# A transformer layer in one kernel: transposes as 12-bit products, and another order table for the attention

## The chip, the cores and the metric

The kernel runs on one core of a Trainium2 chip. A core has five engines that run side by side, each with its own instruction queue, and meet at semaphores: TensorE (PE in the profile; PEld is its weight load), VectorE (DVE), ScalarE (ACT), GpSimd (POOL) and SyncE (SP), which issues DMA transfers. The metric is the device time of one execution in microseconds (us); lower is better. Before the change it is 889.84 us, the median of three runs (888.79 to 892.21).

## The reference

The layer is a "macaron": half a feed-forward network, attention, another half feed-forward network, each on a layer-normalized input and added to the residual. All data is 32-bit.

```python
x = x + 0.5 * ffn(layernorm(x), w_gate, w_up, w_down)
x = x + attention(layernorm(x), Wq, bq, Wk, bk, Wv, bv, Wo, bo)
x = x + 0.5 * ffn(layernorm(x), w_gate, w_up, w_down)
```

x is (2, 1024, 256): two sequences of 1024 tokens with 256 channels. The feed-forward network has 1024 inner channels, silu(x Wg) * (x Wu); of every four neighbours the two largest in magnitude are kept before Wd. The attention is causal, with rotary positions, 32 query heads and 8 key/value heads of 8 channels each, so that four query heads share a key head:

```python
scores = einsum('bhqd,bhkd->bhqk', q, k_rep) / sqrt(8)
scores = where(kpos > qpos, -inf, scores)
out = einsum('bhqk,bhkd->bhqd', softmax(scores), v_rep)
```

## The kernel before

The time has three parts: the first feed-forward network with the projections of the first sequence beside it (up to about 210 us), the attention (to about 715 us), and the second feed-forward network.

**Units and rounds.** The attention works on 16 units, one for each sequence and key head (`units`, L701). A unit has four query heads and 1024 tokens. Each unit goes through two passes, and in round n of the loop `round_` pass 1 of unit n (`cur`) is mixed with pass 2 of unit n-1 (`prev`), and with the preparation of unit n+1 (`nxt`). So both kinds of work are there in rounds 1 to 15; round 0 has no pass 2 and runs beside the last part of the first feed-forward network, and round 16 has no pass 1.

**Precision.** Score products use the format that the kernel calls FR, with 12 bits[...]. To lose nothing, each query and key is split into a high part that the format holds and the remainder (`split`, and L446/L449 in `project`), and both are laid in the rows of one product. Tile `part` holds these parts, typed FR.

**prepare (step prep, L468).** Eight transposes by TensorE turn one unit's 80 columns of `part` (four query heads and a key head, two parts of 8 channels each) into rows, in the PSUM tile `hT`. ACT copies them to `stage`, and SP's DMA queue lays them into the rows of `qT` and `kT`: for each of two strips, zeros into two rows for the maxima, and sixteen copies of parts for both strips together. `qT` and `kT` are in three copies, used in turn.

**pass1 (steps p1, L511).** Score products with queries as rows of the output, `s` at L526, with K = 64 rows so that two heads run at once in the two halves of the array. On the diagonal, the causal mask is added as bf16 products (L534). DVE takes the negated maximum of each row (L546). A step has four heads, or with a second number only one pair of heads. An output of 1024 columns fills the PSUM tile, 128 x 2 x 512.

**negated and shift (neg1, and steps shift, L560).** The maxima are split into two 12-bit parts on POOL (`ms`); four transposes turn them into rows (`mT`, L565), ACT copies them (`mrow`), and four DMA transfers put them into `qT`, so that the score products of pass 2 come out with the maximum already subtracted. shift 0 serves the first half of a unit's queries, shift 1 the second half, in the next round. negated(0) comes after the last p1 step with a number below 4.

**pass2 (steps p2, L579).** Scores again, now with keys as rows (L590). ACT takes the exponential (L599), POOL clears the causal half on the diagonal (L602). **weighted (steps av, L613)** multiplies the exponentials in full 32 bits with the values and a column of ones (L622), summed up in the PSUM tile `av`; after the last step of a half ACT copies it (`oT`, L631). **normalize (steps norm)** transposes `oT` (L640) and divides by the sum of exponentials on DVE. After norm 1 of the last unit of a sequence, `output` applies Wo.

**What sets the order.** PE and POOL run in program order inside the attention (`manual_schedule`); that order is the table `order` (L688), written out by hand as 58 steps. A step number selects a (query tile, key block) in `steps1` or `steps2`. DVE, ACT and SP are ordered by the scheduler from it. Every fourth step of rounds from 1 on, a piece of the second sequence's projection is put in (`second`).

**Buffers.** PSUM has three tiles of two banks in turn (`ps_big`), shared by the p1, p2 and hT tiles and the projections; one of one bank (`ps_tr`) for the other transposes, and one (`ps_acc`) for av. The exponentials have seven buffers (`es`).

A transpose by TensorE takes the data as weights and streams a unit matrix `ident` through them, in 32 bits; its call is `nc.tensor.transpose`.

Of the kernel before, what the change touches and what calls it, by code (L numbers as in the profile page):

```python
# [8 lines left out]
FP = mybir.dt.float32  # L9
BF = mybir.dt.bfloat16  # L10
FR = mybir.dt.float32r
# [5 lines left out]
P = 128  # L17
B, T, C = 2, 1024, 256
NT = B * T
TB = 512  # L20
NTB = NT // TB
NTT = TB // P
# [3 lines left out]
REP = H // NKV  # L26
# [8 lines left out]
def macaron_kernel(  # L35
# [77 lines left out]

    ident = const.tile([P, P], FP, name="ident")
    make_identity(nc, ident)


    half_id = const.tile([P, 2, P], BF, name="half_id")
# [226 lines left out]
    def attention(actx, last, beside_first):  # L345
# [2 lines left out]


        qTs, kTs, vaugs, parts, attns = [], [], [], [], []  # L350
        zeros = ap1.tile([2, TB], FP, name="zeros")
        nc.vector.memset(zeros, 0.0)
        late = {}

# [102 lines left out]
        class Unit:  # L457
# [10 lines left out]
            def prepare(self):  # L468


                s = f"{self.b}_{self.g}"
                tr = ps_big.tile([P, 2, TB], FP, name=f"hT{s}", tag="big")
                src = parts[self.b][:, :, bass.ts(self.g, REP + 1), :].bitcast(FP)
                for t in range(NQT):
                    nc.tensor.transpose(  # L475
                        tr[0 : 2 * GW, t // NTT, bass.ts(t % NTT, P)],
                        src[:, t, :, :].rearrange("p h n -> p (h n)"),
                        ident,
                    )
                hT = ap1.tile([P, T], FP, name=f"stage{s}", tag="stage")  # L480
                nc.scalar.copy(hT[0 : 2 * GW, :], tr[0 : 2 * GW, :, :].rearrange("p i n -> p (i n)"))
                W = 2 * D
                for s in range(2):

                    lo = s * STRIP + ROWS
                    nc.sync.dma_start(
                        out=self.qT[lo : lo + 2, :, :].rearrange("p i (c n) -> p (i c) n", n=TB),
                        in_=zeros[:, None, :].to_broadcast([2, REP, TB]),
                    )
                    for j in range(2):  # L490
                        for i in range(2):
                            lo = s * STRIP + j * W + i * D
                            nc.sync.dma_start(
                                out=self.kT[lo : lo + D, :],
                                in_=hT[REP * W + j * D : REP * W + j * D + D, :],
                            )
                        lo = s * STRIP + j * W
                        for pair in range(2):
                            h = 2 * pair + s
                            nc.sync.dma_start(  # L500
                                out=self.qT[lo : lo + W, pair, :], in_=hT[h * W : h * W + W, :]
                            )
# [57 lines left out]
            def shift(self, half):  # L560
# [1 line left out]
                s = f"{self.b}_{self.g}_{half}"  # L562
                tr = ps_tr.tile([P, TB], FP, name=f"mT{s}", tag="tr")
                for t in range(NTT):
                    nc.tensor.transpose(  # L565
                        tr[0 : 2 * REP, bass.ts(t, P)],
                        self.ms[:, t, :, :].bitcast(FP).rearrange("p i k -> p (i k)"),
                        ident,
                    )
                mT = late["2"].tile([2 * REP, TB], FP, name=f"mrow{s}", tag="mrow")  # L570
                nc.scalar.copy(mT, tr[0 : 2 * REP, :])
# [114 lines left out]


        order = """  # L688
        neg1; p2 0 1; p1 3 1; p2 0 0; av 11; p1 9 0; shift 1; p1 0; p2 1 1; p1 3 0; p2 1 0;
        p1 4 1; norm 1; p2 2; prep; p1 2 1; p2 3; av 0; p2 4 0; p1 7; p2 4 1; av 1; p1 2 0;  # L690
        p2 5 0; p1 1; av 2; p2 5 1; p1 6 0; p2 6 1; av 3; p1 5; shift 0; p1 8 0; p2 6 0;
        p1 8 1; av 4; p2 7 1; p1 10 0; av 5; p2 7 0; p1 9 1; norm 0; p2 8 1; p1 11 0;
        p2 8 0; av 6; p2 9 1; p1 4 0; p2 9 0; av 7; p1 11 1; p2 10; p1 10 1; av 8; p2 11;
        p1 6 1; av 9; av 10
        """
        steps1 = [(qt, kc) for qt in range(NQT) for kc in range(qt // NTT + 1)]
        steps2 = [(qh, kb) for qh in range(2) for kb in range((qh + 1) * NTT)]
# [172 lines left out]
```

## Time and profile before

| | before |
|---|---|
| median of 3 runs | 889.84 us |
| the profiled execution | 894.08 us |
| its span (first to last instruction) | 892.3 us |
| PE busy, share of the span | 848.9 us, 95% |
| DVE busy | 664.8 us, 75% |
| ACT busy | 435.9 us, 49% |
| POOL busy | 220.3 us, 25% |
| mean granted clock of PE | 0.978 |
| hT transposes, 128 records | 19.1 us busy, 296 ns mean |
| mT transposes, 128 records | 19.6 us busy, 277 ns mean |

The profile is of one execution. An engine is busy while an instruction of it is under way. Records of matmuls overlap, since TensorE is a pipeline: a record of 273 ns may be followed by the next after 109 ns, so the time that a product costs is read from the starts of neighbours, not from its length. L12 is line 12 of the kernel before. In `qT<-mrow`, the tile written stands left of the arrow.

### The profile page before, as it was taken

How to read it: one execution, taken by the hardware profiler on the slowest of the kernel's cores; microseconds unless marked ns; L12 is line 12 of the kernel's file. 1: busy time of each engine (PE TensorE's matmuls, PEld its weight loads, DVE VectorE, ACT ScalarE, POOL GpSimd, SP SyncE). 2: the span in 40 equal slices, each digit the busy share in tenths (PEclk: the TensorE clock that was granted, in tenths of full speed). 3: DMA queues.
4: the chain of work that ended last, by engine and by line, in shares of the span. 5: the costliest groups of instructions: out<-in, count | busy, mean ns of one | idle time of the engine just before them, and what ended most of it. 6: DMA issues, size and time to landing. Idle time of an engine off the chain costs nothing.

```text
span 892.3 us, 14666 instructions
## 1 busy us (share of the span) xinstructions
PE 848.9 (95%) x5760; PEld 454.4 (51%) x5760; DVE 664.8 (75%) x927; ACT 435.9 (49%) x570; POOL 220.3 (25%) x405
## 2 busy tenths in 40 slices
PE   5999999898899989999998999999998899999998
PEld 2446664575444454445446444444443444555566
DVE  4797898878777877787885878788883157978682
ACT  1331223202666756777773777777777434212220
POOL 3002376320154433452221222222122200000000
PEclk9999999998899989999998999999998999999999
DMA  8100000201201210221120222112200000000001
GB/s 256 27 0 2 1 1 0 36 14 27 38 14 28 39 27 15 39 35 19 28 39 1 39 39 35 20 28 39 38 3 2 1 1 0 1 12 12 21 3 47
DMA packets 20819, 22.95 MB, mean 26 GB/s; under 512 B 11408, under 2 KB 15888, under 8 KB 20752
## 3 DMA queue, kind: packets, MB, share of 16 engines
q1 hardware_dynamic: 19136, 19.15, 11.6%
q10 hardware_dynamic: 1616, 2.88, 0.9%
q8 instruction: 45, 0.74, 0.4%
q14 instruction: 22, 0.18, 0.1%
HBM read 6.29 MB, written 2.10 MB: 9 GB/s over the span
## 4 chain that ended last, share of the span: by engine, by line
PE 76%; DVE 15%; ACT 4%; POOL 3%; issue 1%; DMA 1%; SPq 1%; ACTq 0%; POOLq 0%
PE gu L229 20%; PE av L622 14%; PE s L590 10%; PE o L284 10%; PE s L526 9%; DVE neg L546 5%; ACT e L599 2%; PE s L534 2%; PE oo L673 2%; PE hT L475 2%; PE otr L640 2%; DVE least L546 2%; PE pr L397 2%; PE mT L565 2%; DVE h L269 1%; PE lnT L180 1%
## 5 line engine op out<-in xcount | busy, mean ns | idle before, releaser
L599 ACT ACTIVATE e<-s 128x1024 f32<-128x1024 f32 (+1 forms) x320 | 291.8, 938 | 136.1 <-PE s L590 123.0
L546 DVE TENSOR_REDUCE least<-s 128x2 f32<-128x1024 f32 (+3 forms) x224 | 251.4, 1144 | 58.3 <-PE s L534 37.2
L622 PE MATMUL av<-e,vaug 128*32 128x512 f32 (+3 forms) x1536 | 162.7, 503 | 1.8 <-ACT oT L631 1.6
L590 PE MATMUL s<-qT,kT 64*128 64x512 f32 (+3 forms) x768 | 151.0, 419 | 9.7 <-DVE neg L546 4.7
L602 POOL TENSOR_SCALAR_AFFINE_SELECT e<-e 128x256 f32<-128x256 f32 (+1 forms) x192 | 94.5, 493 | 257.5 <-ACT e L599 257.2
L526 PE MATMUL s<-kT,qT 64*128 64x512 f32 (+3 forms) x768 | 140.4, 389 | 3.7 <-DVE least L546 1.7
L590 PEld LDWEIGHTS s<-qT,kT 64*128 64x128 f32 x768 | 68.8, 190 | 111.7 <-DVE least L546 40.3
L229 PE MATMUL gu<-xnT,wg_sb 128*128 128x512 f32 x256 | 123.6, 606 | 1.9 <-ACT xnT L187 1.2
L229 PE MATMUL gu<-xnT,wu_sb 128*128 128x512 f32 x256 | 120.5, 593 | 0.0
L546 DVE TENSOR_REDUCE neg<-s 128x2 f32<-128x1024 f32 (+1 forms) x96 | 97.9, 1042 | 28.7 <-PE s L534 26.9
L284 PE MATMUL o<-wd_sb,h 128*128 128x256 f32 x512 | 116.5, 382 | 0.2 <-DVE x L305 0.2
L284 PEld LDWEIGHTS o<-wd_sb,h 128*128 128x128 f32 x512 | 95.8, 190 | 18.4 <-issue 5.1
L526 PEld LDWEIGHTS s<-kT,qT 64*128 64x128 f32 x768 | 69.4, 187 | 58.0 <-ACT e L599 36.3
L237 ACT ACTIVATE sg<-gu 128x512 f32<-128x512 f32 x64 | 38.1, 595 | 111.2 <-PE gu L229 111.2
L240 ACT ACTIVATE a<-h 128x512 f32<-128x512 f32 x64 | 40.3, 630 | 98.1 <-DVE h L239 97.7
L229 PEld LDWEIGHTS gu<-xnT,wu_sb 128*128 128x128 f32 x256 | 49.0, 191 | 62.1 <-issue 62.1
L238 DVE TENSOR_TENSOR sg<-sg,gu 128x512 f32<-128x512 f32 x64 | 43.7, 684 | 48.8 <-ACT sg L237 48.8
L229 PEld LDWEIGHTS gu<-xnT,wg_sb 128*128 128x128 f32 x256 | 48.9, 194 | 56.5 <-issue 49.6
L622 PEld LDWEIGHTS av<-e,vaug 128*32 128x32 f32 x1536 | 32.0, 108 | 49.9 <-issue 26.5
L534 PE MATMUL s<-half_mask,half_id 64*128 64x128 bf16 (+1 forms) x1024 | 56.1, 209 | 0.0
L159 POOL TENSOR_TENSOR rstd<-ve,neg_half 128x4 f32<-128x4 f32 x12 | 12.3, 1025 | 155.4 <-DVE ve L157 155.3
L239 DVE TENSOR_TENSOR h<-sg,gu 128x512 f32<-128x512 f32 x64 | 43.9, 687 | 2.2
(75 smaller groups left out, 679.8 us busy)
## 6 DMA issues: line engine op xcount, KB each, us to landing
qT<-stage SPq DMA_DIRECT2D x128, 64.0 KB
kT<-stage SPq DMA_DIRECT2D x128, 32.0 KB
qT<-mrow SPq DMA_DIRECT2D x128, 4.0 KB
out<-x SPq DMA_DIRECT2D x8, 256.0 KB
wu_sb<-in_wu SPq DMA_DIRECT2D x2, 512.0 KB
wg_sb<-in_wg ACTq DMA_DIRECT2D x2, 512.0 KB
x<-in_x SPq DMA_DIRECT2D x2, 512.0 KB
wd_sb<-in_wd ACTq DMA_DIRECT2D x1, 1024.0 KB
```

The lines of the kernel that those rows point to most:

```text
L229: nc.tensor.matmul(out=gu[:, i, :], lhsT=w_sb[:, kc, gb, j, :], rhs=self.xnT[tb][:, kc, :], start=(kc == 0), stop=(kc == 1),)
L238: nc.vector.tensor_tensor(sg, sg, gu[:, 0, :], ALU.mult)
L239: nc.vector.tensor_tensor(h[:, j, :], sg, gu[:, 1, :], ALU.mult)
L240: nc.scalar.activation(a[:, j, :], h[:, j, :], AF.Abs)
L284: nc.tensor.matmul(out=o[:, i, :], lhsT=self.hms[tb][k // 4][:, k % 4, bass.ts(2 * t2 + i, P)], rhs=wd_sb[:, k // 4, k % 4, :], start=(k = ...
L526: nc.tensor.matmul(out=to[:, i, s, :], lhsT=self.qT[strip, pair, bass.ts(qt, P)].bitcast(FR), rhs=self.kT[strip, bass.ds(kc * TB, n)].bitc ...
L534: nc.tensor.matmul(out=to[:, i, s, n - P + lo : n], lhsT=half_id[strip, half, :], rhs=half_mask[strip, half, lo:], start=False, stop=(half ...
L546: ins = nc.vector.tensor_reduce(dst, to, AX.X, ALU.max, negate=True)
L590: nc.tensor.matmul(out=to[:, i, s, :], lhsT=self.kT[strip, bass.ts(kb, P)].bitcast(FR), rhs=self.qT[strip, pair, bass.ds(q0, n)].bitcast(F ...
L599: nc.scalar.activation(e, to, AF.Exp, scale=SCALE)
L602: nc.gpsimd.affine_select(out=e[:, :, :, 0:P], in_=e[:, :, :, 0:P], pattern=[[0, 2], [0, len(pairs)], [1, P]], compare_op=ALU.is_ge, fill=0.0,
L622: nc.tensor.matmul(out=self.av[32 * i : 32 * i + 32, TB - n : TB], lhsT=vaugs[self.b][:, kb, bass.ds(self.g * (D + 1), 32)], rhs=es[i], st ...
```

## The change

The transposes hT and mT become plain products in the 12-bit format with a unit matrix in that format, `ident_r`, copied once from `ident`. Their data is already rounded to that format, so the product with one is exact. The tile `zeros` shrinks to half its columns, and its DMA repeats it twice as often. The order table has the same 58 steps in another order.

```diff
     ident = const.tile([P, P], FP, name="ident")
     make_identity(nc, ident)
+    ident_r = const.tile([P, P], FR, name="ident_r")
+    nc.vector.tensor_copy(ident_r, ident)
...
-        zeros = ap1.tile([2, TB], FP, name="zeros")
+        zeros = ap1.tile([2, TB // 2], FP, name="zeros")
...
-                src = parts[self.b][:, :, bass.ts(self.g, REP + 1), :].bitcast(FP)
+                src = parts[self.b][:, :, bass.ts(self.g, REP + 1), :]
                 for t in range(NQT):
-                    nc.tensor.transpose(
-                        tr[0 : 2 * GW, t // NTT, bass.ts(t % NTT, P)],
-                        src[:, t, :, :].rearrange("p h n -> p (h n)"),
-                        ident,
+
+                    nc.tensor.matmul(
+                        out=tr[0 : 2 * GW, t // NTT, bass.ts(t % NTT, P)],
+                        lhsT=src[:, t, :, :].rearrange("p h n -> p (h n)"),
+                        rhs=ident_r,
+                        start=True,
+                        stop=True,
                     )
...
-                        out=self.qT[lo : lo + 2, :, :].rearrange("p i (c n) -> p (i c) n", n=TB),
-                        in_=zeros[:, None, :].to_broadcast([2, REP, TB]),
+                        out=self.qT[lo : lo + 2, :, :].rearrange("p i (c n) -> p (i c) n", n=TB // 2),
+                        in_=zeros[:, None, :].to_broadcast([2, 2 * REP, TB // 2]),
...
                 for t in range(NTT):
-                    nc.tensor.transpose(
-                        tr[0 : 2 * REP, bass.ts(t, P)],
-                        self.ms[:, t, :, :].bitcast(FP).rearrange("p i k -> p (i k)"),
-                        ident,
+                    nc.tensor.matmul(
+                        out=tr[0 : 2 * REP, bass.ts(t, P)],
+                        lhsT=self.ms[:, t, :, :].rearrange("p i k -> p (i k)"),
+                        rhs=ident_r,
+                        start=True,
+                        stop=True,
                     )
...
         order = """
-        neg1; p2 0 1; p1 3 1; p2 0 0; av 11; p1 9 0; shift 1; p1 0; p2 1 1; p1 3 0; p2 1 0;
-        p1 4 1; norm 1; p2 2; prep; p1 2 1; p2 3; av 0; p2 4 0; p1 7; p2 4 1; av 1; p1 2 0;
-        p2 5 0; p1 1; av 2; p2 5 1; p1 6 0; p2 6 1; av 3; p1 5; shift 0; p1 8 0; p2 6 0;
-        p1 8 1; av 4; p2 7 1; p1 10 0; av 5; p2 7 0; p1 9 1; norm 0; p2 8 1; p1 11 0;
-        p2 8 0; av 6; p2 9 1; p1 4 0; p2 9 0; av 7; p1 11 1; p2 10; p1 10 1; av 8; p2 11;
-        p1 6 1; av 9; av 10
+        neg1; p2 0 1; p1 1; p2 0 0; av 11; p1 0; shift 1; p1 3 1; p2 1 1; p1 9 0; av 0;
+        p2 1 0; p1 3 0; prep; p1 2 1; p2 2; p1 2 0; p2 3; norm 1; p2 4 0; p1 10 0; p2 4 1;
+        av 1; p1 10 1; p2 5 1; p1 7; p2 5 0; p1 11 0; shift 0; av 2; p2 6 1; p1 9 1; av 3;
+        p1 5; p2 6 0; p1 4 0; av 4; p2 7 1; p1 6 1; p2 7 0; av 5; p1 4 1; p2 8 0; av 6;
+        p2 8 1; p1 8 1; p2 9 0; norm 0; av 7; p2 9 1; p1 11 1; p2 10; av 8; p1 8 0; p2 11;
+        p1 6 0; av 9; av 10
         """
```

## The prediction

> **What bounds the kernel now.** I read the page's busy times first. TensorE (PE) is busy nearly throughout; VectorE (DVE) and ScalarE (ACT) are not.
>
> ```profile
> PE 848.9 (95%) x5760; PEld 454.4 (51%) x5760; DVE 664.8 (75%) x927; ACT 435.9 (49%) x570; POOL 220.3 (25%) x405
> ```
>
> Next, busy time in windows of 28 us over the attention, because the chain of waits repeats there with that period (its reductions at L546 stand at 521.54, 549.51 and 577.47).
>
> ```profile
> core 0: us, PE busy (x) PEld busy (x) DVE busy (x) ACT busy (x) POOL busy (x), PEclk, DMA share, GB/s
> 510.00:538.00 28.00, 27.52 (x288) 13.38 (x280) 22.77 (x26) 20.96 (x25) 6.79 (x17) 1.00 0.20 32
> 538.00:566.00 28.00, 27.51 (x288) 13.38 (x280) 22.79 (x26) 20.96 (x25) 6.81 (x17) 1.00 0.19 33
> 566.00:594.00 28.00, 27.52 (x288) 13.38 (x280) 22.76 (x26) 20.95 (x25) 6.76 (x17) 1.00 0.19 32
> ```
>
> A round of the attention, one pass of the order table, takes 28.0 us. PE has work in flight for 27.5 of it, at the full clock, while DVE has 5 us and ACT 7 us to spare. So a round is set by PE's stream of products and by what holds that stream up. Third, the timeline of one round (columns: start us, length us, engine, line, operation, tiles, count, wait before it):
>
> ```profile
> 535.17 0.39 PE L526 MATMUL s<-kT,qT 64*128 64x512 f32 x2
> 535.49 1.06 PE L622 MATMUL av<-e,vaug 128*32 128x512 f32 x8
> 536.48 0.44 PE L590 MATMUL s<-qT,kT 64*128 64x128 f32 x4
> 536.76 0.45 PE L526 MATMUL s<-kT,qT 64*128 64x512 f32 x2
> ...
> 540.47 0.60 PE L565 MATMUL mT<-ident,ms 128*8 128x128 f32 x4
> 541.00 0.44 PE L526 MATMUL s<-kT,qT 64*128 64x128 f32 x4
> ...
> 542.41 0.44 PE L590 MATMUL s<-qT,kT 64*128 64x384 f32 x2 [0.20 <-DVE neg L546]
> ...
> 544.25 1.07 PE L475 MATMUL hT<-ident,part 128*80 128x128 f32 x8
> 545.25 0.44 PE L526 MATMUL s<-kT,qT 64*128 64x384 f32 x2
> ```
>
> The reader is to see three things. The four mT transposes hold PE from 540.47 to 541.00, 0.53 us: one record is 0.273 long (the view of tile mT, below), so they start (0.60 - 0.273)/3 = 0.109 us apart, and 0.20 passes from the last start to the next product. The eight hT transposes take 1.00 us at the same spacing. And a real wait for a buffer: 542.41, where a p2 tile waits for a reduction.
>
> ```profile
> L565 PEld LDWEIGHTS mT<-ident,ms x128: 82/87/128, 204.5 to 678.7; 128*8 128x8 f32 x128
> L565 PE MATMUL mT<-ident,ms x128: 272/273/417, 204.7 to 678.8; 128*8 128x128 f32 x128
> ```
>
> (Smallest, median and largest duration in ns.) The fourth view is by form, in the draining round (681.75 to 682.0), where score products of 128 columns in the 12-bit format stand with nothing slow behind them:
>
> ```profile
> L590 PE MATMUL s<-qT,kT 64*128 64x128 f32 x4 | 0.3, 246 | 0.0
> ```
>
> They are two pairs (the two halves of the rows run at once); a mean of 246 ns hides 218 for the first pair and 273 for the second, and the pairs start 0.06 us apart (single records: 681.81 and 681.87).
>
> [...] weights of 12-bit products follow each other every 107 to 109 ns. [...]
>
> **The change, part by part.**
>
> *Transposes.* Each unit has 8 hT and 2 x 4 mT. mT now: 3 x 0.109 + 0.20 = 0.53. [...] gain 0.21, twice a unit 0.42. hT: [...] gain 0.31. [...] I take 0.73 us a round[...]. I prefer overlap because the 12-bit pairs at 508.6 and 508.7 start 108 ns apart with 107 ns loads[...].
>
> *Order, on PE.* The table holds the same 58 steps. What differs for PE is how often it goes from half-height products (64 rows, p1 and p2) to full-height ones (av, shift, norm, prep) and back. From the timeline: av follows a 512-column product after 0.32 where a product of its own kind follows after 0.23 (+0.09); the step back costs 0.54 from the last av start where the next av would come after 0.43 (+0.11); and the first half-height product has its weight load in the open (0.334 to the next, against 0.227: +0.107). So a visit costs 0.3. The old table has 16 visits a round (only av 9 and av 10 stand together), the new one 14, since shift 0 stands at av 2 and norm 0 at av 7. With some 0.03 to 0.1 for the change inside the pair I take 0.27 each, 0.54 a round.
>
> *Order, in waits.* The score tiles share three PSUM pairs in turn with hT, so each tile waits until the third before it has been read: by DVE (1.22 us for 1024 columns; 1.13 behind another), or ACT (1.02; 0.92 behind another). I walked both tables through a round with these lengths and the product spacings above (0.23, 0.17, 0.12, 0.11 a pair by width; masks 0.09 or 0.18; av 0.88, 0.67, 0.45, 0.24). The old table gives 27.5 us with 1.3 of waits, the largest at p2 1 0 (0.47; the trace has 0.37 there, the line at 542.41). The missing 0.5 are weight loads that waits leave in the open. The new table has 1.55 of waits, in the stretch from prep to p2 6 0, where only av 1 and the pair shift 0/av 2 break a run of score tiles: p2 2 0.19, p1 2 0 0.30, p1 7 0.17, p2 5 0 0.39. An example: p1 10 1 is done at 10.7 and its reduction, behind p1 10 0's, ends at 12.15; p2 5 0 needs that buffer and PE could start it at 11.8. With the old spacing of the transposes the new table walks at 27.5, as the old one. So the two visits saved are given back to waits, and only with the shorter transposes does the round fall, to 26.8.
>
> Net: 0.73 + 0.54 - about 0.57 given back (0.27 longer waits, and loads left in the open or shared with a wait) = 0.7 us a round. Both tables are complete in rounds 1 to 15: 15 x 0.7 = 10.5. hT of the first unit lies in the FFN, on the path: 0.3. Round 0 is bound by DVE (no exponentials, reductions alone); the draining round by ACT's exponentials and the landing of mrow: nothing, within 2 us either way, also for where norm 1 starts the output of the first sequence. Sum 11.
>
> *The rest at nothing.* The copy of the unit matrix (128 x 128, like attn's 0.29) stands on DVE ahead of xn, where DVE idles 1.21 for rstd; without that cover it costs 0.3 once. Zeros of half the width make twice as many packets on SP's queue, two issues of 0.65 a unit, ahead of shift 0's four mrow issues; those rows are wanted at the next round's start, 14 us later. shift 1's mrow is tighter: its landing is wanted by p2 4 0, 6.3 us after mT in the new table, 6.5 in the old; the trace has the last issue done 3.9 after mT's start, so 0.3 is free with a landing of 2.1. If it were late, everything on PE behind p2 4 0 waits. prep's loads have over 20 us. av 4 needs the copy of av 3's sum (0.59) with three steps between instead of five: it fits with nothing to spare, at most 0.3 a round.
>
> The profiled execution took 894.08 (span 892.3); less 11 it is 883. The median is 4.2 lower: 889.84 - 11 = 879.
>
> **Rivals.**
>
> *The waits do not grow.* DVE has 5 us spare in 28. Then 0.73 + 0.54 = 1.27 x 15 = 19 come through, 870. Against it: the run of score tiles in the middle.
>
> *The waits take it all.* If p2 and p1 in that stretch wait 0.5 more than walked, or loads and products of hT go in turn, a round gains under 0.25: 886 to 890.
>
> *Slower: narrow 12-bit products are slow.* [...] (av, 128 columns: two records of 0.11), the spacing would be 0.215: 16 x 0.106 = 1.7 more a round, 15 rounds 26, so 916. As the order alone gives nothing, it decides from a spacing of 0.109 on; at 0.127 the loss passes 0.5%. Against it: 536.48 to 536.76 holds two narrow pairs and an open load in 0.28.
>
> **How the numbers follow.** Forecast 0.50 (own range 874 to 885); waits not growing 0.22; waits taking all 0.17 (0.03 of it still faster by 0.5%, 0.01 slower); waits beyond the gain, 895 to 900, 0.07; slow narrow products 0.04. Within 0.5% (885.4 to 894.3) is what one measurement cannot tell from no change. Faster: 0.50 + 0.22 + 0.03 = 0.75; same 0.13; slower 0.12. For 8 in 10 I leave out the slower cases and the best part of the full gain: 867 to 890.
>
> **What would show it.** Rounds at 27.3 us (26.7 for the first rival, 29.5 for the third); hT x8 in about 0.75 and mT x4 in 0.38 by the timeline; weight loads of hT near 150 ns, not 119; av starting behind mT and otr with no score product between; waits on p2 5 0 and p1 2 0, and fewer at p2 1 0; the first 200 us as before. I am wrong if hT's spacing exceeds 0.109, if PE waits for av's copy or mrow, or if windows show DVE above 25 of 27.

## The result, and the profile after

The changed kernel takes 878.5 us (median of 6 runs, 875.57 to 883.62), the kernel before 889.32 us (6 runs, 886.97 to 895.08). The ratio is 0.9872, with a 95% interval of 0.9828 to 0.9915: about 11 us faster. Forecast was 879.0, in a range of 867 to 890.

The profiled execution took 876.17 us (span 874.5 us). That is 17.9 us less than the profiled execution of before, more than the medians differ. TensorE's mean clock was 0.987 in this execution and 0.978 in that of before; the last section estimates that the clock can account for the rest. So the two profiles are compared stretch by stretch, not by their ends.

First the page's busy times and granted clock, after:

```profile
PE 830.7 (95%) x5760; PEld 450.9 (52%) x5760; DVE 666.1 (76%) x928; ACT 436.0 (50%) x570; POOL 219.6 (25%) x405
...
PEclk9999999899899999999999999999999999999999
```

TensorE still has work in flight for 95% of the span. It does as many products as before; the number of its busy microseconds fell by 18, those of the other engines changed by less than 2. The kernel is bound as it was.

Second, busy time in windows of one round, cut at the starts of hT:

```profile
core 0: us, PE busy (x) PEld busy (x) DVE busy (x) ACT busy (x) POOL busy (x), PEclk, DMA share, GB/s
504.40:531.54 27.14, 26.73 (x284) 13.47 (x280) 23.03 (x25) 21.00 (x26) 6.68 (x16) 1.00 0.20 33
531.54:558.67 27.13, 26.72 (x285) 13.44 (x281) 23.01 (x25) 21.02 (x26) 6.68 (x16) 1.00 0.20 33
558.67:585.83 27.16, 26.75 (x284) 13.43 (x281) 23.03 (x25) 20.99 (x26) 6.68 (x16) 1.00 0.20 33
```

A round takes 27.14 us at the full clock. Before, cut in the same way, it is 27.96, from the hT at 544.25 that the prediction shows to the next:

```profile
572.21 1.07 PE L475 MATMUL hT<-ident,part 128*80 128x128 f32 x8
```

DVE is busy 23.0 of 27.1, under the 25 of 27 that the prediction named as a sign of error. The gain is 0.82 in such a round. There are 15 rounds, and 15 x 0.82 = 12.3 us, but not all of them are like this one; the part on the change again counts them one by one.

Third, the timeline of TensorE in that round (start us, length us, engine, line, operation, tiles, count, wait before it). Lines moved: hT is L478, mT L570, the p1 scores L531, their masks L539, the p2 scores L597, av L629.

```profile
531.54 0.79 PE L478 MATMUL hT<-ident_r,part 128*80 128x128 f32 x8
532.26 0.44 PE L531 MATMUL s<-kT,qT 64*128 64x384 f32 x2
...
537.44 0.50 PE L531 MATMUL s<-kT,qT 64*128 64x256 f32 x4
537.79 0.34 PE L539 MATMUL s<-half_mask,half_id 64*128 64x128 bf16 x8
538.35 0.50 PE L597 MATMUL s<-qT,kT 64*128 64x512 f32 x2 [0.22 <-DVE least L551]
538.68 0.39 PE L531 MATMUL s<-kT,qT 64*128 64x512 f32 x2
538.92 0.26 PE L539 MATMUL s<-half_mask,half_id 64*128 64x128 bf16 x4
539.11 0.40 PE L570 MATMUL mT<-ident_r,ms 128*8 128x128 f32 x4
539.44 0.64 PE L629 MATMUL av<-e,vaug 128*32 128x256 f32 x8
```

The eight hT products hold TensorE from 531.54 to 532.26, 0.72 us (before: 1.00), the four mT products from 539.11 to 539.44, 0.33 us (before: 0.53). av 2 stands right behind mT, with no score product between. The wait that was at p2 1 0 is gone. In its place stands one at 538.35. The tile p2 5 0, which the prediction named as the place of the largest wait, waits for a reduction of DVE. In this round it is the only one that the timeline gives a releaser to.

Fourth, the records of the two kinds of transposes by tile (smallest, median and largest duration in ns), hT and then mT:

```profile
L478 PEld LDWEIGHTS hT<-ident_r,part x128: 146/152/253, 159.7 to 613.5; 128*80 128x80 f32 x128
L478 PE MATMUL hT<-ident_r,part x128: 232/235/624, 159.8 to 613.5; 128*80 128x128 f32 x128
```

```profile
L570 PEld LDWEIGHTS mT<-ident_r,ms x128: 85/88/130, 205.9 to 663.8; 128*8 128x8 f32 x128
L570 PE MATMUL mT<-ident_r,ms x128: 218/223/411, 205.9 to 663.8; 128*8 128x128 f32 x128
```

The spacing of mT follows as it did before, from the length of a group less that of a record: (0.40 - 0.223)/3 = 0.059. For hT it is read from the starts of single records, which lie 0.072 apart after a first step of 0.124. Before, both had 0.109. A record of hT's weight load is longer than before (152 against 119 ns), while the products follow faster (0.072 against 0.109): the length of a record is not its cost. Of a pair of score products the two records start 4 ns apart (532.261 and 532.265), so the two run at once.

### The profile page after: what moved, and what is told of

It reads as the page before. It is cut to its first block, busy times and chain, and to the rows that moved or that the text cites. A ratio compares the mean times of both kernels' runs of the same rounds, so it can differ in the third digit from the quotient of the medians.

```text
span 874.5 us, 14629 instructions
## 1 busy us (share of the span) xinstructions
PE 830.7 (95%) x5760; PEld 450.9 (52%) x5760; DVE 666.1 (76%) x928; ACT 436.0 (50%) x570; POOL 219.6 (25%) x405
## 3 DMA queue, kind: packets, MB, share of 16 engines
q1 hardware_dynamic: 19392, 19.15, 11.8%
## 4 chain that ended last, share of the span: by engine, by line
PE 81%; DVE 11%; POOL 3%; ACT 2%; issue 1%; DMA 1%; SPq 0%; ACTq 0%; DVEq 0%
PE gu L231 22%; PE av L629 16%; PE s L597 11%; PE o L286 11%; PE s L531 10%; DVE least L551 4%; PE s L539 2%; DVE neg L551 2%; PE otr L647 2%; PE pr L399 2%; PE oo L680 2%; PE lnT L182 1%; ACT e L606 1%; PE mT L570 1%; POOL turn L430 1%
## 5 line engine op out<-in xcount | busy, mean ns | idle before, releaser
L551 DVE TENSOR_REDUCE least<-s 128x2 f32<-128x1024 f32 (+2 forms) x224 | 251.5, 1145 | 56.8 <-PE s L531 36.0
L629 PE MATMUL av<-e,vaug 128*32 128x512 f32 (+3 forms) x1536 | 161.9, 501 | 2.4 <-ACT oT L638 1.4
L597 PE MATMUL s<-qT,kT 64*128 64x512 f32 (+3 forms) x768 | 145.8, 404 | 7.9 <-DVE least L551 3.9
L531 PE MATMUL s<-kT,qT 64*128 64x512 f32 (+3 forms) x768 | 139.4, 386 | 5.6 <-DVE neg L551 2.4
L597 PEld LDWEIGHTS s<-qT,kT 64*128 64x128 f32 x768 | 68.5, 185 | 93.2 <-ACT e L606 29.8
L551 DVE TENSOR_REDUCE neg<-s 128x4 f32<-128x1024 f32 (+2 forms) x96 | 99.9, 1045 | 14.6 <-PE s L539 12.4
L531 PEld LDWEIGHTS s<-kT,qT 64*128 64x128 f32 x768 | 70.2, 187 | 64.6 <-ACT e L606 42.0
L539 PE MATMUL s<-half_mask,half_id 64*128 64x128 bf16 (+1 forms) x1024 | 56.5, 209 | 0.0
L629 PEld LDWEIGHTS av<-e,vaug 128*32 128x32 f32 x1536 | 31.9, 108 | 47.0 <-issue 25.3
L161 POOL TENSOR_TENSOR rstd<-ve,neg_half 128x4 f32<-128x4 f32 x12 | 12.3, 1027 | 154.4 <-DVE ve L159 153.5
```

The costliest lines, as they stand in the source:

```text
L531: nc.tensor.matmul(out=to[:, i, s, :], lhsT=self.qT[strip, pair, bass.ts(qt, P)].bitcast(FR), rhs=self.kT[strip, bass.ds(kc * TB, n)].bitc ...
L539: nc.tensor.matmul(out=to[:, i, s, n - P + lo : n], lhsT=half_id[strip, half, :], rhs=half_mask[strip, half, lo:], start=False, stop=(half ...
L551: ins = nc.vector.tensor_reduce(dst, to, AX.X, ALU.max, negate=True)
L597: nc.tensor.matmul(out=to[:, i, s, :], lhsT=self.kT[strip, bass.ts(kb, P)].bitcast(FR), rhs=self.qT[strip, pair, bass.ds(q0, n)].bitcast(F ...
L629: nc.tensor.matmul(out=self.av[32 * i : 32 * i + 32, TB - n : TB], lhsT=vaugs[self.b][:, kb, bass.ds(self.g * (D + 1), 32)], rhs=es[i], st ...
```

## The experiments

The theory: in a round the products save 0.7 us and the two visits to full-height work about 0.5, of which the table's longer waits take most back, so that the table alone is worth nothing. The rivals: the gain is the table's; or it is neither, but comes from where norm 1, prep and the first round stand. For each kernel there is the median of its runs and the ratio to the runs of before on the same chip, and its **plain round**: the median distance of hT starts over the rounds from about 382 us on that are at full clock and hold no output. In these the projection of the second sequence is done, so that they hold the steps of the table and nothing else. The plain round of before is 27.97. "Due" below means 15 times the gain of a plain round; it is a yardstick, and rounds with other work in them can differ.

### The products alone, and the table alone

The first kernel has the 12-bit products with the old table, the second the new table with the transposes in 32 bits.

```diff
 # the products alone: the changed kernel with the order table of before
-        neg1; p2 0 1; p1 1; p2 0 0; av 11; p1 0; shift 1; p1 3 1; p2 1 1; p1 9 0; av 0;
+        neg1; p2 0 1; p1 3 1; p2 0 0; av 11; p1 9 0; shift 1; p1 0; p2 1 1; p1 3 0; p2 1 0;
...
```

```diff
 # the table alone: the changed kernel with the transposes of before (hT; mT in the same way)
-                    nc.tensor.matmul(
-                        out=tr[0 : 2 * GW, t // NTT, bass.ts(t % NTT, P)],
-                        lhsT=src[:, t, :, :].rearrange("p h n -> p (h n)"),
-                        rhs=ident_r,
-                        start=True,
-                        stop=True,
+                    nc.tensor.transpose(
+                        tr[0 : 2 * GW, t // NTT, bass.ts(t % NTT, P)],
+                        src[:, t, :, :].rearrange("p h n -> p (h n)"),
+                        ident,
```

> The old order table with the twelve-bit products in place of the transposes. Theory (the products carry the gain, the new table is only even): the old table walks at 27.0 us a round with the measured spacings of the products (0.072 for hT, 0.06 for mT) against 27.5 with the old transposes, so a round of 27.5 to 27.6 on the chip against 28.0, 15 rounds, about 6 to 7 us less than before: 883. Rival (the table carries most): under 0.15 us a round, 887 to 890. Rival (the shorter transposes come through in full): 0.65 us a round, 879 to 880.

> The new order table with the old 32-bit transposes; the copy of the unit matrix and the halved zeros stay. Theory: the two visits to full-height products that the new table saves are given back to waits for buffers, so it walks at 27.5 us a round as the old table does, and the time is that of before within 3 us: 887 to 892. Rival (the saved visits come through): 0.5 us a round, 881 to 882. It also bounds the copy of the unit matrix and the zeros, which the theory puts at nothing.

Timeline of TensorE in the products alone, two successive hT:

```profile
540.49 0.79 PE L478 MATMUL hT<-ident_r,part 128*80 128x128 f32 x8
...
567.99 0.79 PE L478 MATMUL hT<-ident_r,part 128*80 128x128 f32 x8
```

The same in the table alone:

```profile
539.48 1.07 PE L477 MATMUL hT<-ident,part 128*80 128x128 f32 x8
...
541.65 0.45 PE L528 MATMUL s<-kT,qT 64*128 64x384 f32 x2 [0.29 <-ACT stage L483]
...
567.32 1.07 PE L477 MATMUL hT<-ident,part 128*80 128x128 f32 x8
```

The rounds are 27.50 and 27.84 long. So in a round:

- the products are worth 27.97 - 27.48 = 0.49 under the old table, and 27.84 - 27.14 = 0.70 under the new one;
- the table is worth 27.97 - 27.84 = 0.13 with the old transposes, and 27.48 - 27.14 = 0.34 with the new ones.

The two help each other by 0.2. The wait in the second fence shows a place where they do: with transposes of 1.0 us, hT is complete 0.28 later, ACT copies it to `stage` that much later, and the third tile behind hT (p1 2 0) has to wait for that copy before it may write there. From hT's start to that tile it is 2.17 us here, and 1.89 in the changed kernel (531.54 to 533.43).

The medians say something else at first. The products alone took 889.17 us (22 runs, ratio 0.9971, 0.9954 to 0.9987), only 2.7 less than before (891.84, 59 runs), where 15 x 0.49 = 7.3 was due. The table alone took 887.18 (22 runs, ratio 0.9947, 0.9932 to 0.9962), 4.7 less, where 15 x 0.13 = 2 was due. The granted clocks close the gap: their means over the runs are 0.9855 for before, 0.9766 for the products alone, 0.9893 for the table alone. A straight line through the 59 runs of before gives 0.70 us for 0.001 of mean clock; through those of the two others 0.67 and 0.79. Moved along its own line to a clock of 0.985, before takes 891.35, the products alone 882.9, the table alone 889.9: gains of 8.5 and 1.4, near the 7.3 and 2 of the rounds. Both lines are extended for this, since the clocks of the products alone lie between 0.972 and 0.981 and those of the table alone between 0.988 and 0.996. That the clock is a cause here, and not only goes along, is tested further down.

### What a visit costs

In the changed kernel shift 0 stands beside av 2, and norm 0 beside av 7. Here a score tile is put between in both places, so that a round has 16 visits again, like the old table.

```diff
-... p1 11 0; shift 0; av 2; ...
+... shift 0; p1 11 0; av 2; ...
-... p2 9 0; norm 0; av 7; ...
+... norm 0; p2 9 0; av 7; ...
```

> The changed kernel with shift 0 one step earlier and norm 0 one step earlier, so that they stand apart from av 2 and av 7 and a round has 16 visits to full-height products again; the order of the score tiles is that of the changed kernel. Theory: a visit costs 0.27 us and nothing hides it, so a round takes 0.53 more, 27.7 against 27.15, and the kernel about 8 us more than the changed one: 886. Rival (the stream has room for it at the waits near by): within 2 us of the changed kernel, 877 to 881.

```profile
539.26 0.79 PE L478 MATMUL hT<-ident_r,part 128*80 128x128 f32 x8
...
566.79 0.79 PE L478 MATMUL hT<-ident_r,part 128*80 128x128 f32 x8
```

The round is 27.54: 0.40 more than the changed kernel's, or 0.20 for each visit. The prediction had 0.27. The wait at p2 5 0 is still there and as long (0.21), and the time came back where the tiles were put: from p2 5 0 to av 2 it is 1.29 (546.05 to 547.34) against 1.09 in the changed kernel (538.35 to 539.44), and from p1 8 1 to av 7, around norm 0, it is 1.29 (555.08 to 556.37) against 1.09 (547.16 to 548.25). So what came back are the visits and not a wait. That also makes the table with 16 visits no better than the old one: 27.54 against 27.48. The median was 889.33 (22 runs, ratio 0.998, 0.9962 to 0.9998), 2.5 us less than before, where 15 x 0.43 = 6.4 was due; the mean clock was 0.9797. At 0.985, along its own line, it is 885.55, a gain of 5.8.

### The change again, and what is left of it without products and table

The changed kernel was run once more beside a kernel that is before with two edits alone: the copy of the unit matrix, and `zeros` of half the width.

```diff
+    ident_r = const.tile([P, P], FR, name="ident_r")
+    nc.vector.tensor_copy(ident_r, ident)
...
-        zeros = ap1.tile([2, TB], FP, name="zeros")
+        zeros = ap1.tile([2, TB // 2], FP, name="zeros")
...
-                        in_=zeros[:, None, :].to_broadcast([2, REP, TB]),
+                        in_=zeros[:, None, :].to_broadcast([2, 2 * REP, TB // 2]),
```

> The changed kernel itself, for a comparison with the other runs on one chip and with the same runs of the kernel before. Every theory expects plain rounds of 27.15 us and 877 to 881.

> The kernel before with only the copy of the unit matrix, which nothing reads, and the halved zeros with their doubled repeats. Theory: both are covered, plain rounds of 27.97 and the time of before within 1 us. Rival (the SP queue's longer transfers hold up mrow): plain rounds longer by 0.1 or more, 2 us or more in all.

The change again: 877.95 us (5 runs, ratio 0.9851, 0.9814 to 0.9888), plain round 27.16, mean clock 0.9844. Before took 890.57 (35 runs) at 0.984, so this pair stands at one clock. The gain is 12.6 us, with an interval of 10.0 to 16.6, too wide to tell 15 x 0.82 = 12.3 from the 10.8 of the first comparison. The two small edits alone: 890.45 (14 runs, ratio 0.9997, 0.9972 to 1.0022), plain round 27.98. They cost nothing that shows, as predicted.

The traces can tell. A mark that stands at nearly the same place in both tables is the mT of shift 1. These are the distances between its starts from one round to the next, for the twelve rounds that are at full clock in all four profiles (us):

| from shift 1 of round | before | products alone | table alone | changed |
|---|---|---|---|---|
| 2 | 34.25 | 33.73 | 34.42 | 33.73 |
| 3 | 27.95 | 27.50 | 27.84 | 27.17 |
| 5 | 30.88 | 30.35 | 31.35 | 30.68 |
| 6 to 8 | 27.95 to 28.00 | 27.45 to 27.47 | 27.81 to 27.84 | 27.14 to 27.17 |
| 10 to 14 | 27.95 to 28.09 | 27.47 to 27.57 | 27.82 to 27.85 | 27.13 to 27.15 |
| 15 (into the draining round) | 25.93 | 25.78 | 27.00 | 26.63 |

The line for round 5, for example, is read from these, before and changed:

```profile
354.12 0.60 PE L565 MATMUL mT<-ident,ms 128*8 128x128 f32 x4
385.00 0.60 PE L565 MATMUL mT<-ident,ms 128*8 128x128 f32 x4
```

```profile
349.04 0.40 PE L570 MATMUL mT<-ident_r,ms 128*8 128x128 f32 x4
379.72 0.41 PE L570 MATMUL mT<-ident_r,ms 128*8 128x128 f32 x4
```

Under the old table the products are worth 0.45 to 0.53 in every round but the last, which has no prep (0.15). The table is not worth the same everywhere: it costs 0.17 in round 2 and 0.47 in round 5, where projections of the second sequence run in between, and 1.07 in round 15. So the changed kernel gains 0.52, 0.78 and 0.20 in rounds 2, 3 and 5, 0.80 to 0.94 in the eight rounds of the next two lines, and loses 0.70 in the last. The other three rounds have some half clock in them and are taken from pairs of kernels with the same amount of it: 0.09 for round 4 (small edits alone 36.31, changed 36.22), 1.09 for round 9 with the output (small edits alone 42.46, against 41.37 in the changed kernel with repeated products, below), and for round 1 1.83 for the table (32.29 and 30.46 in the two kernels with repeated products, below) with some 0.5 for the products, an estimate from the other rounds. Together that is about 11 us, where 15 equal rounds would give 12.3.

### Two other lists

If the walk of the prediction (durations from the trace, three score tiles in turn) is right, then a list that it likes better should be faster. A search with it gave two. For the first the walk gives 26.2 us, where it gives 26.8 for the changed table, and 26.5 to 26.6 was expected on the chip. For the second, chosen with 0.1 added for each weight load in the open behind a wait and each step to full-height products, 26.4 to 26.7 was expected.

```diff
 # the first list
+        neg1; p2 0 1; p1 3 0; p2 0 0; p1 1; shift 1; p2 1 1; p1 7; av 11; p2 2; p1 3 1; av 0;
+        p2 1 0; p1 8 1; prep; norm 1; p2 3; p1 0; p1 11 0; p2 4 0; p2 5 1; av 1; p2 4 1;
+        p1 8 0; av 2; av 3; p1 2 0; p2 5 0; p1 2 1; av 4; p2 6 1; p1 6 0; p2 6 0; av 5; p1 9 0;
+        p2 7 0; p1 11 1; shift 0; p2 8 1; p1 5; norm 0; p2 7 1; p1 10 1; p2 9 0; av 6; p2 8 0;
+        p1 6 1; p2 9 1; av 7; p1 10 0; p2 10; p1 4 1; av 8; p1 4 0; av 9; av 10; p2 11; p1 9 1
```

```diff
 # the second list
+        neg1; p2 0 0; p1 3 0; p2 0 1; p1 10 1; shift 1; p2 1 1; p1 2 1; av 11; p1 0; p1 5; p2 3;
+        prep; p1 1; p2 2; av 0; p2 1 0; p1 2 0; p2 4 0; norm 1; p2 4 1; p1 3 1; av 1; p1 9 0;
+        p2 6 1; p1 10 0; av 2; p2 5 1; p1 7; av 3; shift 0; p1 8 1; p2 5 0; av 4; p1 4 1; p2 6 0;
+        p1 11 0; av 5; p2 8 1; p1 9 1; norm 0; p2 7 0; p1 6 1; p2 7 1; av 6; p2 8 0; p1 11 1;
+        p2 9 0; av 7; p2 9 1; p1 6 0; p2 10; av 8; p1 8 0; p2 11; p1 4 0; av 9; av 10
```

> The changed kernel with another order of the same 58 steps, found by walking many lists with the measured spacings: it has 14 visits (prep and norm 1 together, av 2 and av 3 together, av 9 and av 10 together) and its waits for buffers walk at 1.27 us a round against 1.55. Theory: the walk's 26.2 against 26.8 for the changed kernel holds on the chip, a round of 26.5 to 26.6, 9 us less than the changed kernel: 869. Rival (what the walk leaves out, the landing of transfers and the weight loads after waits, takes it back): 876 or more.

> The changed kernel with a second list of the same 58 steps, chosen with 0.1 us put on each entry from half-height to full-height products and on weight loads after waits, as the first list's trace showed. It has 15 visits and walks at waits of 1.06 us a round against 1.55. Theory (waits and visits together set the round): 0.4 to 0.8 us under the changed kernel's 27.15, so 26.4 to 26.7, some 6 to 10 us less in all: 869 to 873. Rival (the changed table is as good as a list gets, each of these gains goes into weight loads that stand open): 27.0 to 27.3, 877 to 882.

Measured: 27.21 a round and 881.65 us (6 runs, ratio 0.99, 0.9873 to 0.9926) for the first, 27.17 and 878.98 (5 runs, ratio 0.9853, 0.9824 to 0.9882) for the second. Neither beats the changed table's 27.14 to 27.16. The walk was too low by 1.0 for the first list, where it was too low by 0.34 for the changed table and by 0.47 for the old one; the second list came out 0.5 to 0.8 above what was expected. The timeline of the second list at its largest wait:

```profile
557.18 0.49 PE L597 MATMUL s<-qT,kT 64*128 64x512 f32 x2
...
558.04 0.49 PE L531 MATMUL s<-kT,qT 64*128 64x512 f32 x2 [0.36 <-ACT e L606]
```

Here a p1 tile waits 0.36 for an exponential, a kind of wait that the walk knows. The weight loads and entries that it leaves out are not the whole error, since the second list was chosen with a price on them and missed too. What else is missing was not found. A search for the walk's smallest answer can also favour just those lists where its error is largest in that direction; that is argued here, not shown. Both expectations missed.

### Where norm 1 stands

Rounds are not all: the round with the output of the first sequence was 15.65 us longer than a plain one before, and 12.96 in the changed kernel. The table moves norm 1, which starts that output. A rival that gives part of the gain to that: norm 1 moved alone, later, in the kernel of the products alone.

```diff
-... p1 4 1; norm 1; p2 2; prep; p1 2 1; p2 3; av 0; ...
+... p1 4 1; p2 2; prep; p1 2 1; p2 3; norm 1; av 0; ...
```

> The old table with the twelve-bit products, and norm 1 moved from before p2 2 to behind p2 3, where the new table has it (next to av 0, so one visit less). The question is the round in which the first sequence's output is computed: with norm 1 early it took 15.5 us more than a plain round and half of the output's products ran at half the clock; with norm 1 late it took 13.0 more at the full clock. Theory (the place of norm 1 does it): 13.0 to 13.5 here, with no half clock in the output, while plain rounds walk up to 0.4 longer than with norm 1 early, 27.5 to 27.9, since more waits for buffers stand behind the merged visit. Rival (another part of the new table does it, or the clock's phase): 15 to 16 us over a plain round as before.

The output round was indeed short, 12.52 over a plain one. But the plain rounds came out at 28.07, 0.59 longer than with norm 1 in its old place and beyond what was expected, and the kernel took 895.19 us (22 runs, ratio 1.0041, 1.0025 to 1.0057), slower than before. Against before the rounds are only 0.10 longer, 15 x 0.10 = 1.5; the rest of the 4.6 us goes with a mean clock of 0.978 against 0.984. The timeline shows the reason for the longer rounds, ahead of hT:

```profile
541.16 0.50 PE L531 MATMUL s<-kT,qT 64*128 64x512 f32 x2
542.20 0.50 PE L597 MATMUL s<-qT,kT 64*128 64x256 f32 x4 [0.54 <-ACT e L606]
542.63 0.58 PE L478 MATMUL hT<-ident_r,part 128*80 128x128 f32 x5
```

The four transposes of norm 1 stood between these two score tiles (0.60 us of TensorE in the products alone, 539.46 to 540.06). They covered the time until ACT has read an earlier score tile for its exponential, which makes the buffer of p2 2 free; taken away, p2 2 waits 0.54 for it. The visit that norm 1 no longer makes, 0.20, is not enough for that.

That the short output round comes from norm 1's place does not follow, though. Put beside each other by the half clock in that round, the profiles of the old and the new table (and of those that differ from them in one or two places) fall into three classes:

| half clock in the output round | over a plain round | kernels |
|---|---|---|
| none | 12.5 to 13.0 | changed, table alone, changed with 16 visits, norm 1 moved |
| 3.4 us | 14.2 to 14.5 | changed again, its version with repeated products (below), small edits alone, products alone with repeated products (below) |
| 6.8 us | 15.5 to 15.7 | before, products alone |

Windows of before in that round (the column behind POOL's is the granted clock):

```profile
470.60:474.00 3.40, 1.82 (x15) 1.10 (x12) 2.94 (x5) 1.41 (x2) 0.84 (x2) 1.00 0.02 5
474.00:480.80 6.80, 6.12 (x19) 4.49 (x17) 0.86 (x2) 1.17 (x2) 0.00 (x0) 0.51 0.00 0
480.80:484.20 3.40, 2.67 (x16) 2.01 (x15) 2.63 (x10) 0.75 (x2) 0.00 (x0) 0.99 0.00 0
```

TensorE is busy for 1.82 of 3.40 us, and then has half its clock for 6.8, in which DVE is busy for 0.86 and ACT for 1.17: the products of the output are on the path.

Within one table, 3.4 us at half clock go with 1.0 to 1.3 more: 12.96 and 14.2 with the new table, 14.46 to 14.52 and 15.5 to 15.65 with the old one. So of the 2.7 us by which the output round of before was longer in its profile, most go with its 6.8 us at half clock. A part of some 0.3 is left for the table: at the same 3.4 us the old one has 14.46 and 14.52, the new one 14.18 and 14.21. Whether norm 1's place has a share in that is not settled. Of the five profiles with the old table or norm 1 moved in it, four have half clock here, of the five with the new table or its version with 16 visits two; whether the table makes it likelier isn't settled by single profiles. (The two searched lists have no half clock in it, at 13.7 and 13.1.)

### Is the low clock a cause?

In all ten profiles so far, a stretch at half clock of 3.4 to 13.7 us begins between 217 and 221 us. That is where round 0 ends: DVE's reductions set the pace there, and TensorE waits for each. The end of round 0 in the changed kernel, timeline:

```profile
216.12 0.50 PE L531 MATMUL s<-kT,qT 64*128 64x512 f32 x2 [0.91 <-DVE least L551]
...
217.25 0.51 PE L597 MATMUL s<-qT,kT 64*128 64x512 f32 x2 [0.63 <-DVE least L551]
...
218.38 0.97 PE L531 MATMUL s<-kT,qT 64*128 64x256 f32 x4 [0.63 <-DVE least L551]
```

To test it, the last three p1 tiles of round 0 issue their score products four times over; the repeats fall into time in which TensorE waited. This was done in the changed kernel and in the products alone. The 0.4 us for each us at half clock in the first expectation below is an estimate that fits the line of before: 0.001 of mean clock over 890 us is 1.78 us at half clock, and goes with 0.70 us.

```diff
-                for half in range(-1, 2 if diagonal else 0):
+                again = 4 if (self.b, self.g) == (0, 0) and late.get("warm") else 1
+                halves = [-1] * again + list(range(0, 2 if diagonal else 0))
+                for turn, half in enumerate(halves):
...
-                                    stop=not diagonal and pair == pairs[-1],
+                                    stop=(turn < again - 1 or not diagonal) and pair == pairs[-1],
...
-                    next(beside_first, None)
+                    late["warm"] = next(beside_first, 0) == 0
```

> The changed kernel; in round 0, in the last three pass-1 tiles, where TensorE waits 0.6 to 0.9 us per tile for VectorE, the score products are issued four times instead of once (the same result is written again). Theory (the half clock from about 218 us on follows from TensorE's idle time at the end of round 0, and costs 0.4 us for each us of it): the stretch at half clock there, 3.4 to 6.8 us in the changed kernel's profiles, goes or shrinks to 3.4 or less, the mean granted clock rises by 0.002 to 0.004, and the time falls by 1 to 2.5 us against the changed kernel, 876 to 877. Rival (the clock is not moved by this, or other stretches at half clock come in its place): no change within 1 us, or the 2 us of added products shown as a loss.

> The same added products in the kernel with the old table and the twelve-bit products, whose profile has 13.7 us at half clock from 218 on and a mean clock of 0.977 over its runs. Theory: its loss against what its plain rounds give (15 rounds of 0.49 less should be 7 us, measured were 2.6) is the clock's; with the stretch at 218 gone or halved the mean clock rises by 0.003 to 0.008 and the time falls by 2 to 5 us, 884 to 887. Rival (the loss has another cause): 888 to 890 and the same mean clock.

Windows over the end of round 0 and the start of round 1, with the granted clock behind POOL's column again, in the products alone:

```profile
216.00:224.00 8.00, 6.53 (x46) 4.18 (x46) 7.71 (x12) 3.40 (x4) 1.41 (x5) 0.63 0.01 3
224.00:232.00 8.00, 7.70 (x52) 4.37 (x56) 5.48 (x13) 4.47 (x5) 2.91 (x5) 0.52 0.15 25
```

The same with the repeated products:

```profile
216.00:224.00 8.00, 5.66 (x57) 3.33 (x53) 7.93 (x13) 4.13 (x5) 2.03 (x6) 1.00 0.01 2
224.00:232.00 8.00, 6.03 (x77) 3.47 (x78) 6.52 (x14) 4.91 (x6) 2.31 (x3) 1.00 0.27 44
```

The clock of 0.63 and 0.52 became 1.00 and 1.00. In 224 to 232 the second kernel does 77 products in 6.03 busy us, the first 52 in 7.70. Plain rounds did not change (27.47). The products alone went from a ratio of 0.9971 (0.9954 to 0.9987) to 0.9909 (0.9876 to 0.9943), and from a mean clock of 0.9766 to 0.9863: 5.5 us by the ratios, 4.5 by the medians (884.64, 6 runs, though on another chip). So the clock is a cause. In these two profiles that one place is worth 2.4 us: the mT of shift 1 in round 2 starts at 254.27 in the products alone and at 251.89 with the repeats. That is about half of the 4.7 us by which the products alone had fallen short of their rounds. The rest of the gain is not accounted for: stretches at half clock further on, which the edit does not touch, differ between the two profiles as well.

In the changed kernel the same edit gave 877.17 us (6 runs, ratio 0.9835, 0.9798 to 0.9871; clock 0.990). That is the lowest ratio of all kernels here, but the interval overlaps with those of the changed kernel (0.9872 and 0.9851): a gain isn't shown.

## Why the prediction was right

The kernels side by side. The last two columns are 15 times the plain round's gain, and the gain at a mean clock of 0.985, along each kernel's own line of time over clock. That of the changed kernel rests on 5 runs, and those of the products alone and the table alone are extended beyond their clocks.

| | plain round | median us | ratio | 15 x gain | at one clock |
|---|---|---|---|---|---|
| before | 27.97 | 891.84 | 1 | 0 | 0 |
| changed, again | 27.16 | 877.95 | 0.9851 | 12.3 | 12.5 |
| products alone | 27.48 | 889.17 | 0.9971 | 7.3 | 8.5 |
| table alone | 27.84 | 887.18 | 0.9947 | 2.0 | 1.4 |
| changed, 16 visits | 27.54 | 889.33 | 0.998 | 6.4 | 5.8 |
| small edits alone | 27.98 | 890.45 | 0.9997 | 0 | 0.1 |

- **The transposes**, predicted 0.31 for hT and 0.21 twice for mT, 0.73 a round. Measured 1.00 - 0.72 = 0.28 and 0.53 - 0.33 = 0.20 twice, 0.68, and 0.70 as the difference of two kernels under the new table. The gains of 0.31 and 0.21 rested on lengths of load and product for weights of 80 and 8 columns that no trace of before shows; they were the author's assumption. The trace of before has the overlap for score products: a load record of 186 ns from 508.624 lies under the products of 508.517 to 508.842 (the 107 ns of the prediction are the distance from one load to the next). The changed kernel has it for the transposes: hT has 0.072 between products, with load records of 0.152 that start 0.072 apart as well, and mT 0.060. Loads of hT were expected near 150 ns and have 152.
- **The visits**, predicted 0.27 each, 0.54 for two. Measured 0.20, 0.40 for two. This term of the sum was too large by 0.14.
- **What is given back to waits**, predicted 0.57. A gain of 0.82 from 0.70 + 0.40 leaves 0.28. This term was too large by 0.29. The wait at p2 5 0 came where it was placed and in its size: the tile could have started 0.15 after the masks at 537.79, at about 537.95, and starts at 538.35, 0.39 later (predicted 0.39; the timeline itself gives 0.22 of it to the reduction). By the spacings of the prediction p2 2, p1 7 and p1 2 0 start late by about 0.28, 0.24 to 0.34 and 0.17 (predicted 0.19, 0.17, 0.30). The four together came to 1.1 to 1.2, predicted 1.05. So these waits were right as a sum, and the error is in what the prediction set against them: the walk, 0.34 too low for the new table, was 0.47 too low for the old one. Which of the old table's open loads and waits make up that 0.13 was not taken apart.
- **The order alone gives nothing**: it gave 0.13 in a plain round, and costs where projections run in between and in round 15. At one clock that left 1.4 us in all, near nothing as predicted.
- **Net**, predicted 0.7 in each of 15 rounds, 10.5 in all. Measured 0.82 in a plain round, and about 11 over all 15. That the number came out so near is partly luck. Two terms that were both too large had opposite signs, and the 15 rounds, which the prediction took as alike, range from a loss of 0.70 to a gain of about 2.3.
- **Everything outside the rounds "nothing, within 2 us"**: for the changed kernel this holds, since the rounds give about 11 of the 10.8 and 12.6 between the medians. As a bound for any kernel it fails: the products alone fell 4.7 us short of 15 plain rounds, and the version with 16 visits 3.9, at clocks of 0.977 and 0.980, and the prediction did not consider the clock. Had the change been the products alone, its own method would have forecast some 7 and missed.
- **The copy, and zeros**: put at nothing, and the kernel with these alone shows nothing (27.98; 0.9997). The queue has 256 packets more in the changed kernel (19392 against 19136), 8 for each of the 32 transfers of zeros.
- **The rivals.** That waits don't grow would have given 27.97 - 1.27 = 26.7 a round; it is 27.14. That waits take it all would have left over 27.7. That narrow 12-bit products are slow needs a spacing of 0.215, the author's estimate (two records of av, 0.11 each, make 0.22); it is 0.060 and 0.072. (Its rounds would have been 28.0 + 1.7 = 29.7, not the 29.5 that the prediction gives.)
- **The signs.** Rounds were to be 27.3 (27.14), hT about 0.75 and mT 0.38 long in the timeline (0.79 and 0.40), av behind mT with nothing between, no wait at p2 1 0. In rounds 1 to 15 no product of TensorE waits for av's copy or for mrow; in 14 of them weight loads of av stand idle for 0.25 to 0.36 until av's copy, with products in flight meanwhile. The draining round has 1.42 for a copy of av's sum, where before had 1.56, and 0.24 for mrow's landing.

## What to carry to other kernels

Where data is exact in the 12-bit format already, its transpose is cheaper as a product with a unit matrix in that format (0.060 to 0.072 us for 128 columns) than as a 32-bit transpose (0.109), and here, where TensorE sets the time, that came through in full (0.70 of 0.68) under the new table and to 0.49 under the old one. A step that costs TensorE 0.2 us by its place may cover a wait that costs 0.5: before it is moved, look in the timeline for what stands late behind it, and don't trust a search for the smallest answer of a model whose error is as large as the differences it ranks. Compare kernels by a stretch that repeats at the full clock, and put the granted clocks beside the medians, before a few microseconds are given to an edit; but look at the other repeats too before the gain of one is multiplied.

## What the hardware showed unexpectedly

**Half clock in the middle of a busy kernel.** In the traces of before and after, the granted clock is either 1.00 or 0.50. Apart from one that the end of the span cuts off, the profile of before has half clock in six stretches of 3.4, 10.2, 6.8, 6.8, 6.8 and 3.4 us, 37 us in all, the changed kernel's in four, 20 us in all, each a multiple of 3.4. At half clock products take about twice as long: the eight hT of before at 224.70 lie 0.213 apart, where they have 0.109 at the full clock. Half of the 17 us between the two profiles, 8.5, is thus an estimate of the most that this can have cost. The two profiled executions differ by 17.9; the rounds give about 11 of it, and the other 7 fit under that bound.

At the end of round 0 TensorE waited 0.6 to 0.9 us at a time, with score products of half height between. In the changed kernel's profile, by windows, the clock then went to half:

```profile
216.30:217.70 1.40, 0.77 (x4) 0.19 (x3) 1.40 (x2) 0.00 (x0) 0.00 (x0) 1.00 0.00 0
217.70:224.50 6.80, 6.17 (x54) 3.99 (x52) 6.29 (x10) 3.44 (x4) 1.62 (x5) 0.50 0.02 4
224.50:231.00 6.50, 6.07 (x58) 3.14 (x54) 5.61 (x11) 5.14 (x6) 2.69 (x6) 1.00 0.19 30
```

TensorE is in flight for 0.77 of 1.40 us, then at half clock for 6.8. In the ten profiles without repeated products this stretch lasts 3.4 to 13.7 us, although the work of round 1, which comes then, keeps TensorE in flight (6.17 of the 6.80 us above). With repeated products in the gaps the clock was 1.00 from 216 to 232 in the kernel of the products alone, where it had been 0.63 and 0.52. What stays open is why one kernel meets such stretches more often than another: the products alone had a mean clock of 0.977 over 22 runs and the table alone 0.989. The table also sets the order of round 0's p1 steps, so that round does not end alike in both; whether that decides it, no run here tested.

**A shorter transpose has a longer load.** hT's weight loads went from 119 to 152 ns when the transposes became products, and the kernel gained: the loads run under the product before. The load from 531.822 to 531.974, for one, lies under the product from 531.809 to 532.045.
